# Attention in blocks of 30 queries and 55 keys, four blocks and both halves of the heads in parts of TensorE's array

## The chip, the core and the metric

The kernel runs on one core of one Trainium2 chip. The metric is the device time of one execution in microseconds, median of the runs shown. The engines are TensorE (PE in the profile; PEld is its loading of the stationary operand), VectorE (DVE), ScalarE (ACT), GpSimd (POOL) and SyncE (SP), whose queue issues the DMAs.

## The reference

Eight sequences of 512 tokens and 128 channels pass through a block of four stages: a Mamba-like state space stage, a mixture of experts, a chunked attention, and the mixture of experts again, each with its residual. The experts (8 of them, hidden size 512, all computed for every token and weighted by router and gate) are most of the arithmetic. The attention, cut to what matters:

```python
EMBED_DIM, NUM_HEADS, HEAD_DIM = 128, 16, 8
CHUNK_SIZE, LEFT_CONTEXT, RIGHT_CONTEXT = 10, 25, 0
...
chunk_start = i // CHUNK_SIZE * CHUNK_SIZE
in_chunk = (j >= chunk_start) & (j < chunk_end)
in_left = (j >= i - LEFT_CONTEXT) & (j < chunk_start)
# allowed = in_chunk | in_left | in_right; softmax(q k^T * 8 ** -0.5 + mask) v, then W_o
```

So query i sees its own chunk of 10 keys and the keys back to i - 25: a window of at most 35 keys, and a run of n queries that begins at a chunk's start needs n + 25 keys.

## The kernel before, in words

The program is written out by a planner. `Clock` holds an estimate of when each engine is done (`product` gives PE's cost of one matmul, `cost` the others'). `Lanes` holds generators, one per piece of work, and `tick` takes the next piece whose inputs are there by that estimate. `ffn_stream` is the main line: for each sequence and expert it issues the products g, u and y (three matmuls of 128 x 128 x 512 each, on split f32r numbers) on PE, and ACT, DVE and POOL do the work between them. Everything else fits in beside it. The order is fixed when the program is built, and each engine runs its list in that order, with semaphores.

Attention runs beside the experts of the later sequences. `attention_prep` makes q, k and v of a sequence; q and k are cut into three bf16 pieces each and written to DRAM (`put`, tile aqd) in the order of `Q_PIECES` and `K_PIECES`: each entry is one row group of 8 rows (head size), so that one contraction over 64 rows gives the sum of eight products of pieces. `steps` are (sequence, tile) pairs. A tile is about 100 queries and 25 keys more; there are 5 tiles in a sequence (QTILES) and 40 steps. A step has two `units`, each with 4 of the 8 head pairs:

- `load` brings q and k of the step into qs and ks (65 rows: 64 of pieces and one of ones or zeros), `load_values` brings v into vr and DVE copies it to its places in a vtile, 8 columns of a head and 8 of ones in each 32.
- `scores(u)`: for 4 head indices and 2 halves of the heads one matmul each, queries on the output's partitions (tile as). DVE then adds the mask and takes the maximum over the keys, one `tensor_tensor_reduce` per head (amasked), 16 per step.
- `maxima(s)`: POOL cuts the negative maximum in three bf16 pieces, PE transposes them (amt), and three DMAs put them in rows 65 to 67 of qs.
- `weights(u)`: the same products with keys on the partitions and the maximum as three rows more (tile aw). DVE adds the mask (apt), two operations per unit; `exponentials` has ACT apply Exp, four per step.
- `values(s)`: 16 f32 matmuls per step, four at a time beside each other in groups of 32 columns of the array (output partitions 32 j to 32 j + 31), into one bank (ao); the ones beside v give the sums. ACT copies them out, one DMA writes them to DRAM (aod).
- `joined(b, ...)` after the last step of a sequence divides, applies W_o and adds the residual.

`all_loads`, `all_value_loads`, `all_scores`, `all_maxima`, `all_weights`, `all_exponentials` and `all_values` run these per step; `all_scores` lets attention run ahead of the stream's place `pos[0]` by ATT_LEAD. Tiles of 8 PSUM banks are shared: `sides` gives at most OTHERS = 4 to everything but the experts. The profile puts nearly all instructions on line 254, the helper in `Engine` that records them; they are told apart by their tiles.

Of the kernel before, what the change touches and what calls it, by code (L numbers as in the profile page):

```python
# [18 lines left out]
P = 128  # L19
# [25 lines left out]


QTILES = [(0, 110), (110, 100), (210, 100), (310, 100), (410, 102)]
# [3 lines left out]
QROWS = 8 * HD + 1  # L51
KROWS = QROWS + 3
MROWS = 5 * HEADS
# [20 lines left out]
Q_PIECES = (0, 0, 0, 1, 1, 1, 2, 2)  # L74
K_PIECES = (0, 1, 2, 0, 1, 2, 0, 1)
# [42 lines left out]
class Clock:  # L118
# [15 lines left out]
    def product(self, name, out, args):  # L134

        n = size(out)
        if name == "transpose":
            return 0.025 + max(n, 64) / 1540, "square"
        if out.shape[0] == 32:
            return 0.044, "beside"  # L140
        dt = args[1].dtype
        if dt == F32R and n >= 256:
            return n / 2245 + 0.003, "square"
        if dt == BF16:
            return max(n, 64) / 2400 + 0.008, "small" if args[1].shape[0] > 64 else "beside"
        return max(n, 64) * 4 / 2400 + 0.01, "square"

    def cost(self, key, name, out, args, kw):
        n = size(out)
        if key == "T":  # L150
            c, form = self.product(name, out, args)
            was, self.form = self.form, form
            if form != was:
                c += 0.09 * (form == "beside") + 0.09 * (was == "beside") + 0.09 * (form == "square")
            return c
# [195 lines left out]
def block_kernel(ctx: ExitStack, tc: tile.TileContext, x, pack_a, pack_b, pack_c, w_qkv, mask, mask_t, w_o,  # L351
# [97 lines left out]
    maskt = const.tile([QMAX, LEFT + QMAX], F32, name="maskt")  # L449
# [798 lines left out]
    def attention_prep(b, consts):  # L1248
# [7 lines left out]
        for m, (bcol, order) in enumerate(((B_BQ, Q_PIECES), (B_BK, K_PIECES))):  # L1256
# [8 lines left out]
            def put(piece, pi):  # L1265
                js = [j for j, o in enumerate(order) if o == pi]
                places = slice(js[0], js[-1] + 1, js[1] - js[0])
# [45 lines left out]

    steps = [(b, t) for b in range(B) for t in range(len(QTILES))]
    units = [(b, t, i) for b, t in steps for i in range(2)]

    def attention(sb):
        loaded, v_there, maxima_of, scored, maxed, pts, outs, masked = {}, {}, {}, {}, {}, {}, {}, {}

        maskk = sb.tile([KMAX, QMAX + QSTEP], F32, name="maskk")  # L1320
        maskk_there = sp.dma_start(out=maskk, in_=mask_t)
        sp.dma_start(out=maskt, in_=mask)
        wo = sb.tile([P, P], F32, name="wo")
        wo_there = sp.dma_start(out=wo, in_=w_o)
        eye = sb.tile([QMAX, QMAX], BF16, name="eye")

        qss = [sb.tile([KROWS, HEADS, QMAX], BF16, name=f"qs{i}") for i in range(NQS)]
        kss = [sb.tile([KROWS, HEADS, KMAX], BF16, name=f"ks{i}") for i in range(NQS)]
        mps = [sb.tile([QMAX, MROWS // HEADS, HEADS], BF16, name=f"mp{i}") for i in range(2)]

        vtiles = [sb.tile([KMAX, 4 * VPLACE], F32, name=f"v{i}") for i in range(2)]

        def places(v):
            return v.rearrange("p (i c) -> p i c", i=4)[:, :, :P].rearrange("p i (j c) -> p i j c", j=4)

        def constants():
            yield "P"
            pool.tensor_copy(eye, ident[:QMAX, :QMAX])
            for t in kss:
                pool.memset(t[QROWS - 1 :], 1.0)  # L1340
            for t in qss:
                pool.memset(t[QROWS - 1 : QROWS], 0.0)
            for t in mps:
                pool.memset(t[:, 3:], 0.0)
            for v in vtiles:
                pool.memset(v, 0.0)
                pool.memset(places(v)[:, :, :, HD : 2 * HD], 1.0)

        def window(t):
            q0, nq = QTILES[t]  # L1350
            k0 = max(0, q0 - LEFT)
            return q0, nq, k0, q0 + nq - k0

        def load(s):
            b, t = steps[s]
            q0, nq, k0, nk = window(t)
            qd, kd, _, there = heads[b]
            yield "S", there
            qs, ks = qss[s % NQS], kss[s % NQS]
            for h in range(2):  # L1360
                hs = slice(NPAIR * h, NPAIR * h + NPAIR)
                sp.dma_start(out=qs[: QROWS - 1, hs, :nq], in_=qd[h, :, :, q0 : q0 + nq])
                e = sp.dma_start(out=ks[: QROWS - 1, hs, :nk], in_=kd[h, :, :, k0 : k0 + nk])
            loaded[s] = qs, ks, e

        def load_values(s):
            b, t = steps[s]
            _, _, k0, nk = window(t)
            _, _, vd, there = heads[b]
            yield "S", there  # L1370
            vr = sb.tile([KMAX, 4, 4, HD], F32, tag="vr", name=f"avr{s}", bufs=1)
            e = sp.dma_start(out=vr[:nk].rearrange("p i j d -> p (i j d)"), in_=vd[k0 : k0 + nk, :])
            if t == len(QTILES) - 1:
# [3 lines left out]
            dve.tensor_copy(places(vtiles[s % 2])[:nk, :, :, :HD], vr[:nk])  # L1377
            v_there[s] = clock.end["V"] + LAGS["V"]

        def scores(u):  # L1380

            b, t, i = units[u]
            s = u // 2
            q0, nq, k0, nk = window(t)
            qs, ks, there = loaded[s]
            yield "T", there
            both = yield from sides(*(([QMAX, 4, KMAX], f"as{u}_{h}") for h in range(2)))
            for j in range(4):
                for h in range(2):
                    n = NPAIR * h + 4 * i + j  # L1390
                    pe.matmul(
                        both[h][:nq, j, :nk], qs[:QROWS, n, :nq], ks[:QROWS, n, :nk],
                        start=True, stop=True,
                    )
            if i == 0:
                maxima_of[s] = sb.tile([QMAX, HEADS], F32, tag="mx", name=f"amx{s}", bufs=2)
            off = LEFT if t == 0 else 0
            for h in range(2):
                yield "V"
                for j in range(4):  # L1400
                    n = NPAIR * h + 4 * i + j
                    rest = sb.tile([QMAX, KMAX], F32, tag="masked", name=f"amasked{u}_{h}_{j}", bufs=2)
                    e = dve.tensor_tensor_reduce(
                        rest[:nq, :nk], both[h][:nq, j, :nk], maskt[:nq, off : off + nk],
                        -1.0, 3e38, ALU.add, ALU.min, maxima_of[s][:nq, n : n + 1],
                    )
                freed(e)
            scored[u] = e

        def maxima(s):  # L1410

            t = steps[s][1]
            nq = window(t)[1]
            mx = maxima_of.pop(s)
            yield "P", scored[2 * s + 1]
            mp = mps[s % 2]
            rest = sb.tile([QMAX, HEADS], F32, tag="mr", name=f"amr{s}", bufs=1)
            pool.tensor_copy(mp[:nq, 0, :], mx[:nq])
            pool.tensor_tensor(rest[:nq], mx[:nq], mp[:nq, 0, :], ALU.subtract)
            pool.tensor_copy(mp[:nq, 1, :], rest[:nq])  # L1420
            pool.tensor_tensor(mp[:nq, 2, :], rest[:nq], mp[:nq, 1, :], ALU.subtract)
            yield "T"
            tp = yield from side([MROWS, QMAX], f"amt{s}")
            pe.matmul(
                tp[:, :nq], mp[:nq].rearrange("q c h -> q (c h)"), eye[:nq, :nq], start=True, stop=True
            )
            yield "AV"
            mt = sb.tile([3 * HEADS, QMAX], BF16, tag="mt", name=f"amts{s}", bufs=2)
            freed(either(nq)(mt[:, :nq], tp[: 3 * HEADS, :nq]))
            yield "S"  # L1430
            for c in range(3):
                row = QROWS + c
                maxed[s] = sp.dma_start(
                    out=loaded[s][0][row : row + 1, :, :nq], in_=mt[HEADS * c : HEADS * c + HEADS, :nq]
                )

        def weights(u):

            b, t, i = units[u]
            s = u // 2  # L1440
            q0, nq, k0, nk = window(t)
# [3 lines left out]
            both = yield from sides(*(([KMAX, 4 * QMAX], f"aw{u}_{h}") for h in range(2)))  # L1445
            both = [w[:nk, : 4 * nq].rearrange("k (j q) -> k j q", j=4) for w in both]
            for j in range(4):
                for h in range(2):
                    n = NPAIR * h + 4 * i + j
                    pe.matmul(both[h][:, j, :], ks[:, n, :nk], qs[:, n, :nq], start=True, stop=True)  # L1450
            steps_done["w"] = s if i else s - 1
            for h in range(2):
                yield "V"
                pt = sb.tile([KMAX, 4 * QMAX], F32, tag="pt", name=f"apt{u}_{h}", bufs=NPT)
                pt = pt[:nk, : 4 * nq].rearrange("k (j q) -> k j q", j=4)
                k = QMAX if t else 0
                there = freed(dve.tensor_tensor(
                    pt, both[h], maskk[:nk, None, k : k + nq].to_broadcast([nk, 4, nq]), ALU.add
                ))
                masked.setdefault(s, []).append((u, h, pt, there))  # L1460

        def exponentials(s):
            todo = masked.pop(s)
            yield "A", max(there for *_, there in todo)
            for u, h, pt, _ in todo:
                clock.hold = 1e9
                pts[u, h] = pt, act.activation(pt, pt, AF.Exp, scale=scaling)
# [3 lines left out]
        def values(s):  # L1471
# [3 lines left out]
            q0, nq, _, nk = window(t)  # L1475
            v = vtiles[s % 2]
            yield "T", max(v_there[s], *(pts[2 * s + i, h][1] for i in range(2) for h in range(2)))
            o = yield from side([P, 2 * QMAX], f"ao{s}")
            o = o[:, : 2 * nq]
            for i in range(2):  # L1480
                for h in range(2):
                    pt = pts.pop((2 * s + i, h))[0]
                    for j in range(4):
# [239 lines left out]
```

## Time and profile before

| what | value |
|---|---|
| median of 3 runs | 1395.78 us (1392.79 to 1396.54) |
| profiled execution | 1392.73 us, span 1390.9 us |
| mean granted PE clock | 0.988 |
| PE, PEld busy | 1353.4, 1085.0 us |
| DVE, ACT, POOL busy | 1053.2, 963.0, 944.5 us |
| score, weight, output products (as, aw, ao) | 640, 640, 1280 instructions on PE |
| first score product, last output product | 508.9, 1225.4 us after the start |

The table gives the profiled execution, but for its first row. An expert product stands as three matmuls in it. Matmuls overlap: a group's busy time and mean duration count the time from an instruction's start to its modelled end, and the next one starts before that. What a run of matmuls takes of PE's time is read from the start of its first to the start of what follows. The f32 output products have two instructions each in the records.

### The profile page before, as it was taken

To read this page: it belongs to the slowest core of one execution; us is meant where nothing else is said; L and a number is where in the kernel's file an instruction comes from. 1 tells how busy PE (TensorE), PEld (TensorE's weight loads), DVE (VectorE), ACT (ScalarE), POOL (GpSimd) and SP (SyncE) were. 2 spreads that over 40 slices of the span, in tenths; PEclk is the share of its full clock that TensorE was granted. 3 is DMA by queue.
4 is the path that set the end of the run, shared out by engine and by line. 5 is a ranking of instruction groups with operands and counts; after the bars stand their busy time and mean duration, and the time that the engine had idled before them with its cause. 6 is when DMAs were issued, how large, how long until landed. Compare 5 with 4: busy or idle time off the path is not lost. (4 is left out here: it accounts for less than half of the span.)

```text
span 1390.9 us, 25797 instructions
## 1 busy us (share of the span) xinstructions
PE 1353.4 (97%) x8410; PEld 1085.0 (78%) x8410; DVE 1053.2 (76%) x3090; ACT 963.0 (69%) x1671; POOL 944.5 (68%) x1057
## 2 busy tenths in 40 slices
PE   7779999999999999999999999999999999999998
PEld 6677777777778878788788787787887877787886
DVE  6787888888986457888888888888888888754443
ACT  6568768677765557667777677777777776765654
POOL 4667576576674777666767667676666676777776
PEclk9989999999999999999999999999999999999999
DMA  3221214233126223356545455455564545222211
GB/s 123 73 82 35 69 39 125 59 81 91 35 54 81 55 52 65 84 110 125 129 88 125 100 117 137 78 128 115 105 141 78 116 64 100 53 66 53 39 39 38
DMA packets 256631, 116.28 MB, mean 84 GB/s; under 512 B 107996, under 2 KB 252401, under 8 KB 256497
## 3 DMA queue, kind: packets, MB, share of 16 engines
q1 hardware_dynamic: 256497, 114.64, 38.1%
q8 instruction: 66, 1.08, 0.3%
q14 instruction: 68, 0.56, 0.1%
HBM read 82.22 MB, written 31.98 MB: 82 GB/s over the span
## 5 line engine op out<-in xcount | busy, mean ns | idle before, releaser
L254 POOL TENSOR_TENSOR h<-h,h 128x512 fp32r<-128x512 f32 (+1 forms) x510 | 642.1, 1267 | 278.6 <-ACT h L254 242.5
L254 PE MATMUL u<-xt_f,wu 128*128 128x512 f32 (+1 forms) x1584 | 458.7, 398 | 10.3 <-ACT h L254 4.5
L254 PE MATMUL g<-xt_f,wg 128*128 128x512 f32 (+1 forms) x1584 | 454.4, 395 | 4.1 <-DVE mst L254 3.3
L254 PE MATMUL y<-h,wd 128*128 128x512 f32 (+1 forms) x1584 | 450.5, 394 | 1.9 <-POOL h L254 1.9
L254 ACT CAST h<-h 128x512 fp32r<-128x512 f32 (+1 forms) x476 | 286.4, 605 | 224.6 <-DVE h L254 222.3
L254 DVE TENSOR_TENSOR h<-u,h 128x512 f32<-128x512 f32 (+1 forms) x438 | 292.5, 673 | 180.3 <-PE u L254 126.0
L254 ACT ACTIVATE h<-g 128x512 f32<-128x512 f32 (+1 forms) x528 | 305.1, 583 | 116.2 <-PE g L254 90.2
L254 PEld LDWEIGHTS y<-h,wd 128*128 128x128 f32 x1584 | 290.9, 190 | 70.8 <-POOL h L254 3.0
L254 PEld LDWEIGHTS g<-xt_f,wg 128*128 128x128 f32 x1584 | 288.6, 190 | 70.2 <-DVE mst L254 4.0
L254 PEld LDWEIGHTS u<-xt_f,wu 128*128 128x128 f32 x1584 | 284.7, 189 | 74.9 <-ACT h L254 8.0
L254 POOL TENSOR_TENSOR acc<-acc,cwb 128x512 f32<-128x512 f32 (+1 forms) x115 | 146.9, 1278 | 54.9 <-DVE cwb L254 28.3
L254 DVE CUSTOM_DVE_ANT_0 amasked<-as,maskt 100x125 f32<-100x125 f32 (+2 forms) x640 | 141.6, 278 | 11.4 <-PE as L254 10.9
L254 ACT ACT_TABLE_LOAD x102 | 130.9, 1283 | 16.3 <-PE g L254 14.9
L254 DVE TENSOR_TENSOR apt<-aw,maskk 125x400 f32<-125x400 f32 (+2 forms) x160 | 89.7, 574 | 12.5 <-PE aw L254 12.4
L254 DVE TENSOR_TENSOR cwb<-y,cwb 128x512 f32<-128x512 f32 (+1 forms) x115 | 77.3, 672 | 16.6 <-PE y L254 9.6
L254 ACT ACTIVATE apt<-apt 125x400 f32<-125x400 f32 (+2 forms) x160 | 80.8, 540 | 0.4
L254 DVE SCALAR_TENSOR_TENSOR h<-h,g 128x512 f32<-128x512 f32 (+1 forms) x90 | 58.4, 651 | 18.4 <-ACT h L254 18.2
L254 DVE SCALAR_TENSOR_TENSOR h<-u,h 128x512 f32<-128x512 f32 (+1 forms) x90 | 58.8, 655 | 3.8
L254 PEld LDWEIGHTS <-ks 68*125 68x125 bf16 (+2 forms) x640 | 47.2, 136 | 11.4 <-issue 2.1
L254 PEld LDWEIGHTS <-qs 65*100 65x100 bf16 (+2 forms) x640 | 45.4, 125 | 11.0 <-issue 0.5
L254 DVE DVE_READ_ACCUMULATOR2_ANT amx<- 100x1 f32 (+2 forms) x640 | 51.5, 80 | 0.0
L254 PE MATMUL aw<-qs,ks 68*125 68x100 bf16 (+2 forms) x640 | 49.2, 220 | 0.5 <-DMA qs<-amts 0.5
(195 smaller groups left out, 1241.6 us busy)
## 6 DMA issues: line engine op xcount, KB each, us to landing
cwb<-cwd_f SPq DMA_DIRECT2D x124, 256.0 KB
aqd<-apc SPq DMA_DIRECT2D x64, 192.0 KB
ks<-aqd SPq DMA_DIRECT2D x48, 125.0 KB
qs<-aqd SPq DMA_DIRECT2D x48, 100.0 KB
x_fo<-x SPq DMA_DIRECT2D x16, 256.0 KB
aqd<-apc SPq DMA_DIRECT2D x32, 128.0 KB
x_f<-x SPq DMA_DIRECT2D x15, 256.0 KB
aod<-aos SPq DMA_DIRECT2D x24, 100.0 KB
```

The lines of the kernel that those rows point to most:

```text
L254: f(*args, **kw)
```

## The change

Attention is cut into blocks of 30 queries and 55 keys. A step has four blocks, that is 120 queries; a sequence has four such steps and a last one with the remaining 32 queries and 57 keys as one block (STEPS). There are no units: a step does all 16 heads at once. The eight pieces of the contraction become six (48 rows instead of 64), three rows for the maximum follow directly (51 rows), and the two halves of the heads lie on partitions 0 to 50 and 64 to 114 of the same qs and ks. Then:

- Scores: 64 matmuls per full step. Each has 48 rows (half h of the heads at row 64 h) and 32 columns (block i at column 32 i), and 57 keys stream through it. The output has block i on partitions 32 i, all 8 head pairs side by side, one bank for each half. DVE's masked maximum takes 128 partitions x 57, 16 per full step and 4 in the last.
- Maxima: two DMAs instead of three (four in the last step); the POOL operations and the transpose take 128 partitions.
- Weights: 64 matmuls per full step, 51 rows x 64 columns (keys of block 2 a + i at column 64 i), 30 queries streaming. DVE's mask addition and ACT's Exp are one operation of 128 x 480 for each half of the heads, two per step instead of four.
- Values: 64 f32 matmuls per full step, 64 rows (the block's keys) x 32 columns, 30 queries streaming, into two banks, one per half of the rows; two copies by ACT. The last step has 16. v is loaded by four DMAs per step, one per block, and copied by one DVE operation on 128 x 256.
- The masks are small tiles, the first step's own copies having the missing keys filled by POOL; ks, vr and vtiles are filled as a whole at the start.
- The planner's costs of matmuls in parts of the array, and of the change between forms, are other numbers.

The diff, cut to its core:

```diff
-QTILES = [(0, 110), (110, 100), (210, 100), (310, 100), (410, 102)]
-QROWS = 8 * HD + 1
+STEPS = [(0, 4), (120, 4), (240, 4), (360, 4), (480, 1)]
+BQ, BQ_MAX = 30, 32
+BK = 64
+BK_MAX = LEFT + BQ_MAX
+QROWS = 6 * HD
 KROWS = QROWS + 3
...
-Q_PIECES = (0, 0, 0, 1, 1, 1, 2, 2)
-K_PIECES = (0, 1, 2, 0, 1, 2, 0, 1)
+Q_PIECES = (2, 1, 0, 0, 0, 1)
+K_PIECES = (0, 0, 0, 1, 2, 1)
...
-        if out.shape[0] == 32:
-            return 0.044, "beside"
         dt = args[1].dtype
+        rows, cols = args[1].shape
+        if rows <= 64 or cols <= 64:
+            if dt == BF16:
+                return 0.006 if cols <= 32 else 0.012, "beside"
+            return 0.0135 if rows <= 64 else n * 0.00053, "beside"
...
-                c += 0.09 * (form == "beside") + 0.09 * (was == "beside") + 0.09 * (form == "square")
+                c += 0.09 * (form == "beside") + 0.02 * (was == "beside") + 0.09 * (form == "square")
...
             for t in kss:
-                pool.memset(t[QROWS - 1 :], 1.0)
-            for t in qss:
-                pool.memset(t[QROWS - 1 : QROWS], 0.0)
+                yield "P"
+                pool.memset(t, 0.0)
+                for h in range(2):
+                    pool.memset(t[64 * h + 32 : 64 * h + 64], 1.0)
...
             for h in range(2):
-                hs = slice(NPAIR * h, NPAIR * h + NPAIR)
-                sp.dma_start(out=qs[: QROWS - 1, hs, :nq], in_=qd[h, :, :, q0 : q0 + nq])
-                e = sp.dma_start(out=ks[: QROWS - 1, hs, :nk], in_=kd[h, :, :, k0 : k0 + nk])
+                rows = slice(64 * h, 64 * h + QROWS)
+                sp.dma_start(out=qs[rows, :, :nq], in_=qd[h, :, :, q0 : q0 + nq])
+                e = sp.dma_start(out=ks[rows, :, k0:nk], in_=kd[h, :, :, q0 - LEFT + k0 : q0 - LEFT + nk])
...
-            vr = sb.tile([KMAX, 4, 4, HD], F32, tag="vr", name=f"avr{s}", bufs=1)
-            e = sp.dma_start(out=vr[:nk].rearrange("p i j d -> p (i j d)"), in_=vd[k0 : k0 + nk, :])
+            for i in range(blocks):
+                k0 = q0 + BQ * i - LEFT
+                n = max(0, -k0)
+                r = BK * (i % 2)
+                e = sp.dma_start(out=vr[r + n : r + nk, i // 2, :], in_=vd[k0 + n : k0 + nk, :])
...
-            both = yield from sides(*(([QMAX, 4, KMAX], f"as{u}_{h}") for h in range(2)))
-            for j in range(4):
+            both = yield from sides(*(([P, NPAIR, BK_MAX], f"as{s}_{h}") for h in range(2)))
+            n = NPAIR if blocks > 1 else 2
+            for m in range(n):
                 for h in range(2):
-                    n = NPAIR * h + 4 * i + j
-                    pe.matmul(
-                        both[h][:nq, j, :nk], qs[:QROWS, n, :nq], ks[:QROWS, n, :nk],
-                        start=True, stop=True,
-                    )
+                    rows = slice(64 * h, 64 * h + QROWS)
+                    for i in range(4):
+                        k, q = (m, BQ * i) if blocks > 1 else (2 * i + m, 0)
+                        pe.matmul(
+                            both[h][32 * i : 32 * i + BQ_MAX, m, :],
+                            qs[rows, k, q : q + BQ_MAX], ks[rows, k, q : q + BK_MAX],
+                            start=True, stop=True,
+                        )
...
-            for c in range(3):
-                row = QROWS + c
-                maxed[s] = sp.dma_start(
-                    out=loaded[s][0][row : row + 1, :, :nq], in_=mt[HEADS * c : HEADS * c + HEADS, :nq]
-                )
+            for h in range(2):
+                rows = loaded[s][0][64 * h + QROWS : 64 * h + KROWS]
+                first = 3 * n * h
+                if blocks > 1:
+                    maxed[s] = sp.dma_start(
+                        out=rows[:, :, : 4 * bq], in_=mt[first : first + 3 * n].rearrange("x i r -> x (i r)")
+                    )
+                    continue
...
-            both = yield from sides(*(([KMAX, 4 * QMAX], f"aw{u}_{h}") for h in range(2)))
-            for j in range(4):
-                for h in range(2):
-                    n = NPAIR * h + 4 * i + j
-                    pe.matmul(both[h][:, j, :], ks[:, n, :nk], qs[:, n, :nq], start=True, stop=True)
+            both = yield from sides(*(([P, 2 * NPAIR * BQ], f"aw{s}_{h}") for h in range(2)))
+            for m in range(NPAIR):
+                for a in range(pairs):
+                    for h in range(2):
+                        rows = slice(64 * h, 64 * h + KROWS)
+                        for i in range(min(blocks, 2)):
+                            q = bq * (2 * a + i)
+                            pe.matmul(
+                                both[h][BK * i : BK * i + nk, a, m, :],
+                                ks[rows, m, q : q + nk], qs[rows, m, q : q + bq],
+                                start=True, stop=True,
+                            )
...
-            o = yield from side([P, 2 * QMAX], f"ao{s}")
+            o = yield from sides(*(([P, 4 * BQ], f"ao{s}_{i}") for i in range(each)))
             for i in range(2):
-                for h in range(2):
-                    pt = pts.pop((2 * s + i, h))[0]
-                    for j in range(4):
-                        c = 2 * VPLACE * i + P * h + 32 * j
-                        e = pe.matmul(
-                            o[32 * j : 32 * j + 32, i * nq : i * nq + nq], v[:nk, c : c + 32], pt[:, j, :],
-                            start=(h == 0), stop=(h == 1),
-                        )
-                    lanes.give("pt", e)
+                for a in range(pairs):
+                    for h in range(2):
+                        for k in range(each):
+                            rows = slice(BK * k, BK * k + nk)
+                            for j in range(4):
+                                c = VPLACE * (4 * a + 2 * i) + P * h + 32 * j
+                                e = pe.matmul(
+                                    o[k][32 * j : 32 * j + 32, i, a, :],
+                                    v[rows, c : c + 32], pts[s, h][0][rows, a, 4 * i + j, :],
+                                    start=(h == 0), stop=(h == 1),
+                                )
```

## The prediction

> **What bounds the kernel now.** The page first. TensorE (PE) is busy in nearly every slice, at the full granted clock after the first ones.
>
> ```profile
> PE 1353.4 (97%) x8410; PEld 1085.0 (78%) x8410; DVE 1053.2 (76%) x3090; ACT 963.0 (69%) x1671; POOL 944.5 (68%) x1057
> PE   7779999999999999999999999999999999999998
> PEclk9989999999999999999999999999999999999999
> ```
>
> A busy PE need not be a bound one, so the table of stages comes next, for 620 to 1210 us, where attention runs beside the expert products:
>
> ```profile
> 620.00:1210.00 590.00, 589.83 (x4492) 474.45 (x4490) 491.66 (x1835) 432.74 (x745) 405.82 (x494) 1.00 0.52 106
> ```
>
> PE has no idle time there (589.83 of 590); DVE stands at 83%, ACT at 73%, POOL at 69%, the DMA engines at 0.52. The waits of PE agree: the longest in the whole run are start-up ones, and attention makes PE wait in one place only.
>
> ```profile
> PE u L254 <- ACT h L254: 4.5, 4, 2.2
> PE u L254 <- DVE mst L254: 4.3, 1, 4.3
> ...
> PE aw L254 <- DMA qs<-amts: 0.5, 2, 0.3
> ```
>
> So a microsecond of PE removed between 509 us (the first score product) and 1226 us (the last output copy) is a microsecond of span. The chain that ended last only names the final transposes and tells nothing here. What an attention product costs PE is not its mean duration, since products overlap. It is read from starts in the timeline of PE:
>
> ```profile
> 706.70 0.86 PE L254 MATMUL y<-h,wd 128*128 128x512 f32 x3
> 707.40 0.86 PE L254 MATMUL g<-xt_f,wg 128*128 128x512 f32 x3
> 708.09 0.60 PE L254 MATMUL as<-ks,qs 65*100 65x125 bf16 x8
> 708.51 0.95 PE L254 MATMUL u<-xt_f,wu 128*128 128x512 f32 x3
> 709.30 0.86 PE L254 MATMUL y<-h,wd 128*128 128x512 f32 x3
> 710.09 0.91 PE L254 MATMUL ao<-apt,v 127*32 127x102 f32 x32
> 710.92 0.61 PE L254 MATMUL aw<-qs,ks 68*110 68x110 bf16 x8
> 711.36 0.95 PE L254 MATMUL g<-xt_f,wg 128*128 128x512 f32 x3
> 712.14 0.86 PE L254 MATMUL u<-xt_f,wu 128*128 128x512 f32 x3
> ```
>
> Three expert products take 0.70 us (706.70 to 707.40). Eight scores take 0.42 (708.09 to 708.51), and the group behind them 0.79 instead of 0.70: 0.51 in all. Eight weights take 0.44 plus 0.08: 0.52. The output products cost 0.09 before they start (709.30 to 710.09 is 0.79), 0.83 themselves, and by the same pattern 0.09 behind: 1.01.
>
> **PE before.** A step (about 102 queries) has two runs of scores, two of weights, one of outputs: 2 x 0.51 + 2 x 0.52 + 1.01 = 3.07 us; five steps a batch are 15.35. Runs that follow each other directly, as the 32 and the 8 at 710.09, share a 0.09; I judge that for a quarter of the 25 runs, 0.55 us. So 14.8 us a batch, 118 us over eight batches.
>
> **PE after.** A step is 120 queries, four per batch, and a fifth of 32. A full step has 64 scores (48 rows x 32 columns, 57 streamed), 64 weights (51 rows x 64 columns, 30 streamed), and 64 output products (64 rows x 32 columns, f32, 30 streamed), which count as 128 since the f32 outputs stand in the trace with two instructions each (1280 for 640). So 256 tiny products take the place of 64 recorded before, in three runs instead of five. What does one cost? The trace has output products in four column parts, and the Mamba product mde in two row halves:
>
> ```profile
> 710.09 0.30 PE L254 MATMUL ao<-apt,v 127*32 127x102 f32 x4
> 710.09 0.36 PE L254 MATMUL ao<-apt,v 127*32 127x102 f32 x5
> 150.25 0.49 PE L254 MATMUL mde<-mxb,wdt 64*128 64x256 f32 x2
> ```
>
> Four products begin and end in 0.30 us where one lasts 0.275 (mean of the window's four): they start some 8 ns apart; the trace's exact starts give 7. The two mde, 480 ns each, start within 10 ns. Column parts and row halves thus do run beside each other. A group of four ao comes every 0.09 us, which is the 102 columns streaming in each part. With 30 columns a part is free after 0.09 x 30 / 102 = 0.026 us, and four starts at 7 ns fill that time: scores and outputs are then set by the 7 ns, whether all eight parts overlap or only four.
>
> Scores: 64 x 7 ns = 0.45. Outputs: 128 x 7 = 0.90. Weights have four parts, each with 64 columns to load. From below 7 ns. From above, load and stream one after the other in a part: 0.44 us / 8 = 55 ns for an aw product with 110 loaded columns bounds the load of 64 at 32 ns, the stream takes 26 ns as above, and 58 ns over four parts is 14 ns. In the aw rows load and stream overlap (55 ns, not twice that), so I take 9.4 ns, nearer the lower end: 0.60.
> Fixed cost of a run in parts: 0.09 before; 0.83 less eight groups of 0.09 is 0.11 for the first load and the change back; 0.09 on the group behind: 0.3 each. Before, scores and weights paid only the last 0.09; the change adds 0.2 to each of those runs.
> A full step: 0.75 + 0.90 + 1.20 = 2.85. The last step (16 scores, 16 weights in two row halves at 18 ns, 32 outputs): 0.41 + 0.59 + 0.52 = 1.52. A batch: 4 x 2.85 + 1.52 = 12.92, less 0.34 for runs that share: 12.6. Against 14.8 that is 2.2 us a batch, **18 us** in all.
>
> A rule speaks against this. The Trainium skill, "TensorEngine Tiling (Array Packing)", Instruction Overhead, gives each matmul some 60 cycles however few columns it has, and warns against taking the parts from a dimension that is already small, as the 30 columns here. By an estimate from that page's figure (25 ns at 2.4 GHz), paid in series, the 1088 products of a batch would take 27 us, and the kernel would be about 130 us slower. The same skill's "TensorE: Matmul & The Clock Gate", Part 3, has parts start some 4 ns apart, and the rows above (7 to 8 ns) side with it, for four at a time.
>
> **The rest.** DVE: 640 masked reductions at 278 + 80 ns become 544 on 57 elements; 110 elements took 265 and 125 took 282, so some 205 + 80: 229 us become 155. The mask additions (160 x 574) become 64 x some 650 and 16 x some 420: 92 to 48. ACT's exponentials (160 x 540) become 64 x some 590 and 16 x 430: 86 to 45; output copies become 72 smaller ones, 5 us more. None is credited: PE waits for none of them. Value loads grow from one to four per step, the maxima's shrink from three to two, so SP issues 11 instead of 9; behind them stand cwb's broadcasts, but PE's waits on DMAs total 0.5 us, so I cost this at nothing; without that cover a late landing costs up to that order per step, 0.3 x 40 = 12 us. The fills of POOL (ks, qs, v) ran near 435 us, 70 us before the first score; larger tiles there cost a few us of POOL, bounded by 10, hidden by that lead. Two banks for an output step instead of one: ACT's copies (0.33 us) free them soon; nothing.
>
> The profiled execution took 1392.73 us (span 1390.9); 18 less is 1374.7. The median of the runs shown, 1395.78, is 3 us above it, so the forecast is **1378**. Own range: weights at 7 ns and runs at 0.25 fixed, 28 us gained (1368); weights at 14 ns, 7 us gained (1389).
>
> **Rivals.**
> Slower: the 7 ns hold for a handful of products but not for a run of 64 or 128. The longest run in parts today is 32 products in 0.83 us, 26 ns each on the average, so no row shows PE's sequencer feeding 128 weight loads and products in 0.45 us. Place: all three runs. At a common spacing s a batch is 1088 s + 4.16 us (15 runs at 0.3, less 0.34); it equals 14.8 at s = 9.8 ns, and each further ns costs 8.7 us. At 13 ns: +28 us, 1424. At 26 ns: +141, 1537. For it: nothing excludes it. Against: in ao the spacing is that of the streaming columns, not of the feed.
> Doesn't do what it says: weights in parts do not overlap load with stream, runs cost more on entry: gain 0 to 7, 1389 to 1396.
> Another engine becomes the bound: DVE, ACT and POOL were at 83, 73 and 69% and none but POOL gets more work, so the gain would be kept; I give it no time of its own. More than 28 us gained needs a spacing below 7 ns.
>
> **Chances.** Forecast (1368 to 1389) 0.62; larger gain 0.07; little or none (1389 to 1396) 0.09, of which 0.05 is within 0.3%; slower 0.22, 0.13 of it beyond 1420. About 0.3% (4 us) is what a measurement of this kernel can tell from none. Faster 0.73, same 0.05, slower 0.22. The range 1363 to 1420 leaves out 0.05 below and 0.13 above.
>
> **What would show it.** Scores: a run of 64 as in 0.40 to 0.50 us from start to start; aw 64 in 0.45 to 0.9; ao 128 in 0.85 to 1.0; three expert products still 0.70; PE busy throughout 620 to 1200 with waits as small as now; DVE some 110 us less busy. Wrong if the as run takes over 0.65 us (10 ns each), or if PE shows waits on DMA, DVE or ACT in the attention stage.

## The result, and the profile after

The changed kernel took 1417.32 us (median of 4 runs, 1413.14 to 1419.71) against 1395.28: a ratio of 1.0157, 95% interval 1.0127 to 1.0188. A second series of the same program later gave 1408.94 us, 1.0099 (1.0073 to 1.0124). It is slower, where faster was forecast; the first median lies inside the stated range, at its upper end. The profiled execution has a span of 1411.3 us, 20.4 more than before. Three executions among those of the experiments below (two of the block-diagonal kernel, one of the kernel with outputs in one run) took 2.6 to 4.4 ms and stand in no figure.

The page after, the lines of PE's busy share and clock, and of the queue that brings PE its instructions (packets, MB, share of time); the single line behind them is the same queue before:

```profile
PE 1357.9 (96%) x14556; PEld 1071.0 (76%) x14556; DVE 959.0 (68%) x2800; ACT 921.7 (65%) x1608; POOL 942.6 (67%) x1055
PEclk8989999999999999999999999999999999999999
q8 instruction: 114, 1.87, 0.5%
```

```profile
q8 instruction: 66, 1.08, 0.3%
```

PE has 29112 instructions now (products and weight loads), 16820 before. Divided by the packets this is 255 in both kernels, and every packet has 16 KB: q8 carries PE's own instructions, in blocks of some 256. The table of stages for the same stretch as before, and the waits of PE:

```profile
620.00:1210.00 590.00, 574.72 (x9450) 447.45 (x9449) 394.24 (x1547) 381.67 (x665) 389.31 (x467) 0.99 0.43 98
```

```profile
PE ao L263 <- issue: 9.4, 8, 3.0
PE as L263 <- issue: 4.1, 3, 2.4
PE y L263 <- issue: 3.2, 1, 3.2
```

PE was idle for 0.2 us of these 590 before, and for 15 now. The waits are new, and the profile names no engine and no DMA for them: "issue". All other engines are less busy than before, so none of them has become the bound.

The timeline of PE shows where they lie. A clean run of scores and one of outputs:

```profile
821.60 0.86 PE L263 MATMUL g<-xt_f,wg 128*128 128x512 f32 x3
822.39 0.68 PE L263 MATMUL as<-ks,qs 48*32 48x57 bf16 x64
822.99 0.97 PE L263 MATMUL u<-xt_f,wu 128*128 128x512 f32 x3
823.80 0.86 PE L263 MATMUL y<-h,wd 128*128 128x512 f32 x3
...
825.20 0.86 PE L263 MATMUL u<-xt_f,wu 128*128 128x512 f32 x3
826.00 1.29 PE L263 MATMUL ao<-apt,v 64*32 64x30 f32 x128
827.21 0.96 PE L263 MATMUL y<-h,wd 128*128 128x512 f32 x3
828.01 0.87 PE L263 MATMUL g<-xt_f,wg 128*128 128x512 f32 x3
```

Scores cost 0.79 - 0.70 before, 0.60 themselves, 0.81 - 0.70 behind: 0.80 us. Outputs cost 0.10 + 1.21 + 0.10: 1.41. Many runs look like this. Others stop in the middle, and what follows a long stop is slow:

```profile
624.14 0.90 PE L263 MATMUL ao<-apt,v 64*32 64x30 f32 x83
628.07 0.65 PE L263 MATMUL ao<-apt,v 64*32 64x30 f32 x45 [3.03 <-issue]
628.65 1.65 PE L263 MATMUL u<-xt_f,wu 128*128 128x512 f32 x3
630.10 1.48 PE L263 MATMUL y<-h,wd 128*128 128x512 f32 x3
```

```profile
628.00:632.00 4.00, 3.93 (x54) 3.19 (x54) 0.69 (x1) 0.88 (x2) 0.20 (x2) 0.57 0.18 62
```

The run has issued 83 of its 128 instructions when PE falls idle for 3 us. The next three expert products take 1.45 us instead of 0.70, and the granted clock of that stretch is 0.57. In this trace the four longest stops, and no other, are followed by a stretch of half clock, of 3.4 or 6.8 us. In the trace's exact times there are 12 stops over 0.4 us inside or directly behind attention runs; beyond the normal spacing they add 17.9 us, the half-clock stretches 7.1 (both nil before). Another 2.8 us had been lost before the first score product, for a reason that stays open (the repeat below did not lose them). Of 20.4 us that leaves 7 us gained by the shorter runs.

Each of the 12 stops ends 1.3 to 1.6 us after the end of a 16 KB packet on q8, for instance 624.85 to 628.07 with a packet from 625.7 to 626.7, 1049.36 to 1052.73 with one from 1050.4 to 1051.3. Counted in PE's products and weight loads, the stops lie whole multiples of 254.3 instructions apart, to within 4: each comes at the end of a block. This gave the theory tested below.

**Theory A**: PE's instructions arrive in blocks of 256. A run in parts uses up a block faster than the next one arrives, so PE stops until it has come. **Theory B**: the parts of the array, or the banks and semaphores of these products, make PE stop. **Theory C**: SP's longer queue makes PE wait for DMAs (the maxima).

### The profile page after: what moved, and what is told of

It reads as the page before. It is cut to its first block, busy times and chain, and to the rows that moved or that the text cites. A ratio compares the mean times of both kernels' runs of the same rounds, so it can differ in the third digit from the quotient of the medians.

```text
span 1411.3 us, 37837 instructions
## 1 busy us (share of the span) xinstructions
PE 1357.9 (96%) x14556; PEld 1071.0 (76%) x14556; DVE 959.0 (68%) x2800; ACT 921.7 (65%) x1608; POOL 942.6 (67%) x1055
## 5 line engine op out<-in xcount | busy, mean ns | idle before, releaser
L263 DVE TENSOR_TENSOR h<-u,h 128x512 f32<-128x512 f32 (+1 forms) x475 | 318.6, 675 | 268.0 <-PE u L263 192.0
L263 DVE CUSTOM_DVE_ANT_0 amasked<-as,maskq 128x57 f32<-128x57 f32 x544 | 80.6, 214 | 22.3 <-PE as L263 22.0
L263 PEld LDWEIGHTS ao<-apt,v 64*32 64x32 f32 (+1 forms) x4352 | 42.0, 105 | 24.9 <-issue 22.7
L263 PE MATMUL ao<-apt,v 64*32 64x30 f32 (+1 forms) x4352 | 47.5, 199 | 9.4 <-issue 9.4
L263 DVE TENSOR_TENSOR apt<-aw,maskk 128x480 f32<-128x480 f32 x64 | 39.9, 650 | 9.3 <-PE aw L263 9.1
L263 DVE DVE_READ_ACCUMULATOR2_ANT amx<- 128x1 f32 x544 | 45.0, 83 | 0.0
L263 ACT ACTIVATE apt<-apt 128x480 f32<-128x480 f32 (+1 forms) x80 | 44.7, 562 | 0.4
L263 DVE SCALAR_TENSOR_TENSOR h<-h,g 128x512 f32<-128x512 f32 (+1 forms) x53 | 33.0, 626 | 16.6 <-ACT h L263 16.4
L263 DVE CAST h<-h 128x512 fp32r<-128x512 f32 (+1 forms) x67 | 35.8, 536 | 1.1
L263 DVE SCALAR_TENSOR_TENSOR h<-u,h 128x512 f32<-128x512 f32 (+1 forms) x53 | 33.0, 627 | 2.1
```

What stands on the lines that cost most here:

```text
L263: f(*args, **kw)
```

## The experiments

"Stops" are gaps over 0.4 us from start to start in or directly behind runs of as, aw, ao (and the added products), less 0.1 us each, from the traces' exact starts, where the profile puts the wait down to issue; gaps that it puts down to a DMA or another engine are not in the column. All 59 stops of the table end 1.2 to 1.6 us after the end of a 16 KB packet on q8. Nine more of the same kind, over 0.6 us and between other products, are not counted: two in the shifted kernel, three with runs 0.8 us apart, one each with bf16 and block-diagonal outputs, two with the burst. "Half clock" is what expert products took beyond 0.233 us each in slow stretches, whatever stood before them. Both are between 500 and 1300 us.

| kernel | time, us | ratio to before (95%) | stops, us | half clock, us |
|---|---|---|---|---|
| before | 1395.28 | 1 | 0 | 0 |
| changed | 1417.32 | 1.0157 (1.0127 to 1.0188) | 17.9 | 7.1 |
| changed, again | 1408.94 | 1.0099 (1.0073 to 1.0124) | 20.6 | 7.2 |
| shifted by half a block | 1422.3 | 1.0204 (1.0167 to 1.0241) | 21.3 | 10.4 |
| runs 2.5 us apart, outputs in two | 1396.17 | 1.0013 (1.0001 to 1.0026) | 0 | 0 |
| runs 2.5 us apart, outputs in one | 1403.87 | 1.0088 (1.0064 to 1.0113) | 10.0 | 3.2 |
| runs 0.8 us apart, outputs in two | 1419.54, one run | none | 7.4 | 5.3 |
| outputs in bf16 | 1376.7 | 0.9887 (0.984 to 0.9934) | 2.6 | 3.7 |
| block-diagonal outputs | 1401.64 | 1.0056 (1.0032 to 1.0079) | 2.0 | 6.7 |
| before, with a burst added | 1489.3 | 1.0674 (1.0632 to 1.0717) | 17.1 | 7.9 |
| block-diagonal, 2.5 us apart | 1381.26 | 0.9907 (0.9892 to 0.9921) | 0 | 0.2 |
| bf16, 2.5 us apart | 1370.87 | 0.9833 (0.9815 to 0.9851) | 3.8 | 1.7 |

Each ratio is to runs of the kernel before from the same series (medians 1393.79 to 1395.28).

### The same products, further apart

```diff
+        def spaced():
+            while clock.now < burst[0] + SPACE:      # SPACE = 2.5
+                yield "T", burst[0] + SPACE - TO_PE
...
             yield "T", there
+            yield from spaced()                      # scores; weights and values alike
...
             for i in range(2):
+                if i and pairs > 1:                  # values: a second run
+                    burst[0] = clock.end["T"]
+                    yield "T"
+                    yield from spaced()
```

> The changed kernel with the same products, but each run in parts begins at least 2.5 us after the end of the one before, and the 128 output instructions of a full step come in two runs of 64 instead of one. Theory A (PE's instructions arrive in blocks, and a run that uses them up faster than they arrive stops until the next block lands): the pauses inside the runs, which PE's waits put down to issue (16.7 us in the changed kernel's trace, 26 us with the half-clock stretches behind them), fall under 5 us; the extra run costs 32 x 0.3 = 10 us; so about 1413 - 24 + 10 = 1399 us. Theory B (the parts of the array themselves stop now and then, by a change of form or a conflict of their accesses): the pauses stay at 15 us or more, and the time is about 1413 + 10 = 1423.

It took 1396.17 us, and the stops are gone. The table of stages:

```profile
620.00:1210.00 590.00, 589.43 (x9596) 453.35 (x9596) 410.60 (x1590) 393.59 (x688) 399.00 (x483) 1.00 0.44 99
```

PE is busy for 589.43 of 590 us again, with the same products in the same parts. They do not stop the array by themselves, which refutes theory B; they stop it when they come too close. The gain of the shorter runs is spent on the 32 extra ones, so that the time equals that before the change.

### The same program, and one shifted by half a block

```diff
+        for i in range(32):
+            j = 32 * (i % 4)
+            nc.tensor.matmul(
+                warm[j : j + 32, HALF : HALF + 30], ident[:, j : j + 32], ident[:, :30], start=True, stop=True
+            )
```

These f32 products have two instructions and two weight loads each: 128 PE instructions, at the start.

> The changed kernel itself once more, for how far the places of its pauses repeat. Theory A: most long pauses (over 0.4 us) at the same products as in the first trace, since the block's ends fall on the same instructions, with lengths that differ with the fetch; 1412 to 1420 us. Theory B expects the same, so this run only gives the measure for the shifted one.

> The changed kernel with 32 small products (64 instructions and 64 weight loads) more at the very start, outside the planner's clock, which shift every later PE instruction by half a block of 256; all else is issued in the same order. Theory A (a pause comes where a block's end falls into a run): about as many pauses in total, 15 to 30 us with their half-clock stretches and 1408 to 1422 us, but in other steps: at most a third of the long pauses (over 0.4 us) in the same products as in the changed kernel's trace. Theory B (the pauses belong to products, banks or semaphores): the same places as in the changed kernel's trace.

The repeat had 9 long stops, each in the same step and behind the same instruction as one of the first trace's 12. The shifted kernel had 11, and none behind the same instruction. In three runs of outputs both stopped, and there the place had moved by exactly 64 of the run's instructions (with their 64 weight loads, the half block). The run of one step, from the first trace, the repeat and the shifted kernel:

```profile
715.03 0.67 PE L263 MATMUL ao<-apt,v 64*32 64x30 f32 x55
716.26 0.92 PE L263 MATMUL ao<-apt,v 64*32 64x30 f32 x73 [0.57 <-issue]
```

```profile
712.63 0.67 PE L263 MATMUL ao<-apt,v 64*32 64x30 f32 x55
713.88 0.91 PE L263 MATMUL ao<-apt,v 64*32 64x30 f32 x73 [0.58 <-issue]
```

```profile
717.33 1.20 PE L263 MATMUL ao<-apt,v 64*32 64x30 f32 x119
720.12 0.27 PE L263 MATMUL ao<-apt,v 64*32 64x30 f32 x9 [1.59 <-issue]
```

55 twice, then 55 + 64 = 119. Data, banks and semaphores were the same in all three; only the place in the instruction stream differed. So theory A holds for where PE stops. How long it stops differs from run to run, and the time with it.

### How close is too close

The spread kernel with outputs in one run of 256 PE instructions, and the spread kernel with `SPACE = 0.8`:

```diff
             for i in range(2):
-                if i and pairs > 1:
-                    burst[0] = clock.end["T"]
-                    yield "T"
-                    yield from spaced()
```

> As the spread kernel (runs at least 2.5 us apart), but the outputs of a full step in one run of 128 products, which is 256 PE instructions with the weight loads, just the size of one fetched block of 16 KB. Theory A with about one block in hand when the next is asked for: a run of a whole block still meets a boundary each time and pauses in some steps: pauses of 5 to 12 us in output runs and none in scores and weights; 10 us less for the extra runs saved: about 1393 to 1400. If two or more blocks were in hand, no pauses, and about 1386.

> As the spread kernel with outputs in two runs, but runs only 0.8 us apart instead of 2.5: five runs of 128 PE instructions can follow within 4 us. Theory A: a block takes about 2.6 us from its packet's start to its first instruction, so runs this close pause again where several follow each other: 3 to 10 us of pauses put down to issue, 1398 to 1408 us. Theory B: as spread, the pauses depend on nothing that spacing changes; none seen there, none here: 1396.

```profile
PE ao L264 <- issue: 6.4, 4, 2.5
...
PE as L264 <- issue: 2.5, 2, 2.1
```

The lines are the waits of the kernel with outputs in one run. With runs of a whole block 10.0 us of the 17.9 us of stops come back, even 2.5 us from the next run, though not only in outputs as expected, and the time is above the expected 1393 to 1400. Runs of half a block 0.8 us apart stop too (7.4 us). Their one execution, 1419.54 us, is above what was expected; its waits on the maxima's DMAs had grown as well, and three stops of the same kind lay between expert products, so it shows the stops' return and not their price:

```profile
PE aw L264 <- DMA qs<-amts: 3.8, 5, 1.9
...
PE u L264 <- issue: 2.9, 2, 1.9
...
PE y L264 <- issue: 1.3, 1, 1.3
```

### Fewer instructions for the outputs

Outputs with one instruction each instead of two:

```diff
-                pts[s, h] = pt, act.activation(pt, pt, AF.Exp, scale=scaling)
+                pb16 = sb.tile([P, 2 * NPAIR * BQ], BF16, tag="pt16", name=f"apu{s}_{h}", bufs=NPT)
...
+                pts[s, h] = pb16, act.activation(pb16, pt, AF.Exp, scale=scaling)
```

> The changed kernel with the exponentials and v rounded to bf16 for the output products, which then have one instruction each instead of two: 128 PE instructions less in each full step, the same products in the same parts. Theory A: the output run falls from 1.44 to about 0.8 us (32 x 0.6 + 8 x 0.2 = 21 us) and the pauses to under 8 us, with the half-clock stretches some 18 us less: about 1374. Theory B (pauses go with the number of products and parts): pauses fall only by the output instructions' share, to about 11 us: about 1385, with pauses still in output runs.

1376.7 us, as A expected; one stop of 2.6 us, in a run of scores, below B's 11 and not in outputs. Another wait, which neither expectation has, is larger:

```profile
PE aw L263 <- DMA qs<-amts: 8.1, 9, 2.6
...
PE as L263 <- issue: 2.5, 1, 2.5
```

Row halves of the outputs undone (not shown: NPT, the number of tiles for the exponentials, falls from 5 to 3, and exponentials wait for the outputs of the step before):

```diff
+                    pd = pds[h]                      # zeros off the diagonal
+                    for k in range(2):
+                        rows = slice(BK * k, BK * k + BK)
+                        e = act.activation(pd[rows, :, :, k, :], pt[rows], AF.Exp, scale=scaling)
...
+                                o[32 * j : 32 * j + 32, i, a, :], v[:nk, c : c + 32], p,   # 128 rows, 60 queries
```

> The changed kernel with the row halves of the output products undone: two blocks' exponentials stand block-diagonally with zeros beside them, so one product of 128 rows x 32 columns streams 60 queries for both blocks; 32 products (64 instructions) per full step instead of 64 (128), in one bank; ACT has two exponentials of 64 partitions for each half of the heads instead of one of 128. Scores and weights stay as changed. Theory A: output run about 0.8 + 0.3 = 1.1 us instead of 1.44 (11 us over the run), pauses under 8 us: about 1383, faster than the kernel before the change by 10 us or more. Theory B (row halves cause the pauses): pauses vanish in output runs and stay in scores and weights: about 1390.

1401.64 us, a miss: the output run has about the expected length (1.07 + 0.10 us against 1.1) and the stops fell to 2.0 us, but a wait stands in their place:

```profile
PE aw L263 <- DMA qs<-amts: 10.5, 6, 4.0
...
PE aw L263 <- issue: 1.9, 1, 1.9
```

PE now comes to the weights before the maxima have landed. At these six waits the two DMAs of a step start some 0.85 us after each other, the first 1.4 to 7.4 us after ACT or DVE has written amts: SP comes to them late. In the bf16 kernel the same wait was 8.1 us, in the changed kernel 0.6. So theory C is no cause of the change's loss, but becomes one as soon as PE is faster. The one stop in weights and none in outputs would fit this run's theory B as well; against B stands the spread kernel, whose outputs have the row halves and do not stop.

### The burst by itself

The kernel before, with 64 products of the changed form behind each step's outputs:

```diff
+            d = yield from sides(*(([P, 8, 32], f"ad{s}_{k}") for k in range(2)))
+            for part in range(8):
+                for k in range(2):
+                    for j in range(4):
+                        e = pe.matmul(
+                            d[k][32 * j : 32 * j + 32, part, :30],
+                            ident[64 * k : 64 * k + 64, 32 * j : 32 * j + 32], ident[64 * k : 64 * k + 64, :30],
+                            start=True, stop=True,
+                        )
```

> The kernel before, with 64 extra products of the changed form (64 rows x 32 columns, f32, 30 streamed: 128 instructions and 128 weight loads) directly behind each step's output products; they read constants and nothing uses them. Theory A: 40 x (128 x 8.3 ns + 0.1) = 47 us for the products, plus pauses put down to issue as in the changed kernel, since a step then issues about as many PE instructions as the changed one: 10 to 25 us with their half-clock stretches; 1450 to 1465. Theory B by dependences or planner (pauses come from the attention's own data): no pauses in these products, about 1441.

```profile
PE ad L254 <- issue: 13.0, 8, 2.6
...
PE aw L254 <- issue: 3.2, 2, 1.9
```

1489.3 us, above the expected 1465. Products that wait for no attention data stop in the same way: 17.1 us in all, 13.7 of them in the added products, and 7.9 at half clock behind. The price of a burst without a stop is near what was expected, 1.22 us from its start to what follows (9.5 ns each, against 8.3 and 0.1 us on top), 49 us for the 40. Of the 86.9 us by which this trace is longer than that of the kernel before, some 13 are left: the change of form between outputs of 128 rows and products of 64, which was not counted, the waits on the maxima's DMAs (3.3 us, 0.5 before) and the two stops elsewhere; their shares were not told apart.

### A version faster than both

Block-diagonal outputs, runs 2.5 us apart, and the maxima planned later:

```diff
-            yield "T", maxed[s]
+            yield "T", maxed[s] + 2.5
```

> The block-diagonal outputs again (64 output instructions per full step), with runs in parts at least 2.5 us apart and the planner told that the maxima land 2.5 us later, so that PE does not come to the weights before them. Theory A (instructions arrive in blocks): with the pauses (7.7 us in runs, and 16 us of waits on the maxima's DMAs and half-clock stretches in its trace, where the kernel before has 3 and 5 us) gone, about 1399 - 15 = 1384 us, 10 us faster than the kernel before the change. Theory B (the parts themselves stop): no change against 1400. Theory C (the waits on the maxima's DMAs cost as much as the pauses and come from SP's longer queue): they vanish with the margin, same time as A.

> The bf16 output products with runs in parts at least 2.5 us apart and the maxima planned 2.5 us later; outputs in one run of 128 PE instructions. Theory A: no run uses more than half a block at a time, pauses under 3 us, half-clock stretches gone: about 1377 - 13 = 1364 us. Theory B: no change against 1377.

The block-diagonal kernel took 1381.26 us, the bf16 one 1370.87. The first has full f32 outputs and is 0.9907 of the kernel before (0.9892 to 0.9921). Its stops fell from 2.0 us to none and its waits on the maxima's DMAs from 10.5 to none, by two edits at once, so what each edit did (A and C) was not told apart; of the two terms the waits were the larger. The bf16 kernel kept 3.8 us of stops where under 3 were expected: two runs of 128 instructions stopped 2.3 and 3.7 us behind the run before, so half a block at that distance stops seldom, but can stop.

## Why the prediction was wrong

**The bound.** Right: PE had no slack and the other engines did; DVE got 94 us less busy of some 110 forecast, without effect. Each microsecond of PE counted, the lost ones too.

**The prices of the runs.** Scores 0.80 us against 0.75 forecast, weights 0.82 against 0.90, outputs 1.41 against 1.20, the last step about 1.5 against 1.52. A full step is 3.03 instead of 2.85, a batch 13.3 us instead of 12.6, against 14.8 before: 12 us of gain where 18 were forecast. Added up over the whole trace, with entry and exit and without the stops, attention takes PE some 110 us, and 118 before, as the prediction had it: 8 us, near the 7 us that the account of the span left. Entry and exit costs were as read from the trace of before. The output term was too small because 7 ns does not hold through a run: some 30 scores start within 0.11 us (3.4 ns each), and from there on one comes every 8.3 ns, that is 4.2 ns for each of its product and its weight load. The outputs, with 128, pay this longest.

**The step that failed** is the one that priced a run as its number of instructions times one spacing, with nothing for their supply. The slower rival had the right place and the wrong form: it expected one larger spacing throughout, deciding above 9.8 ns. The steady spacing is 8.3 ns and alone would have left a gain. What turned it into a loss is the block: in place of the nothing that the sum had for the supply, the trace has 12 stops of 17.9 us and 7.1 us of half clock behind the longest. The page before had the number, 66 packets on the instruction queue for 16820 instructions, and the change's own count gives what follows: a full step has 256 products, each with its load, 512 instructions in three runs, two blocks in some 3 us of PE time.

The Trainium skill, "Runtime: NRT & Kernel Launch", Instruction fetch mechanics, states that instructions come in blocks of 256 and that the next is fetched while the current one executes, mostly hidden, since engines issue more slowly than blocks arrive. The blocks agree with the packet counts here; that the fetch is hidden does not hold for these runs. The rule weighed in the prediction (some 60 cycles for each product) does not hold for products in parts: the spread kernel's 64 scores take 0.6 us, not 1.6.

**What was costed at nothing.** SP's two more DMAs per step were hidden in the changed kernel (0.6 us of waits) but not in the faster versions (8.1 and 10.5 us), within the 12 us named for an absent cover. Whether the added DMAs or the order of SP's queue makes them late was not tested. POOL's fills and ACT's extra copies cost nothing that the waits show.

## What to carry to other kernels

When a change splits few large PE instructions into many small ones, count the instructions as well as the cycles, and look in the profile at the instruction queue: a run that uses a block of 256 instructions faster than the next comes (here 2.2 to 2.9 us from a packet's start to the end of the stop) can stop PE. Half clock followed 22 of the 25 stops of the table with 2 us or more from start to start, and 2 of the 34 shorter ones. Keep such runs to half a block, with longer work between them, or lower the instruction count first: half the output instructions, 2.5 us of distance and a later plan for the maxima turned 1.6% slower into 0.9% faster. A wait that the profile puts down to issue, and that moves when unrelated instructions are added ahead, points to the instruction supply.

## What was not expected of the hardware

- In a run of scores PE took 4.2 ns per instruction in the long part and about 1.7 (3.4 ns for a product and its load) in the first 30 products, with a pause of 0.1 us between; no run before the change could show it.
- Stops stay behind the same instruction from execution to execution (9 of 9 in the repeat), though their lengths vary: one took 2.0 us in the first trace and 4.8 in the repeat.
- When the packet that ends a stop started, PE was already past the end of the block before, by as little as 0.04 of a block at short stops and by a whole one at the longest two: no more than one block seems to be in hand. What delays the packet (at 1049.36 until a microsecond into the stop) stays open.
